# A complex product by three real products in the first spectral layer of an attention + Fourier block

## The chip, the cores and the metric

The kernel runs on one core of a Trainium2 chip. The core has a matrix engine (TensorE, PE in the profile), a vector engine (VectorE, DVE), a scalar engine (ScalarE, ACT), a general engine (GpSimd, POOL) and a queue that starts transfers (SyncE, SP). Each runs its own list of instructions in order, and they wait for each other by semaphores. Matrix products land in PSUM[...]. The metric is the device time of one execution in microseconds (us), lower is better. All times are medians over runs, except where a profiled execution is named.

## The reference

The input is an image of 48 x 48 positions with 768 channels, in float32. A transformer block (attention over all 2304 positions, then a two-layer perceptron) is followed by a spectral layer, and only that layer is touched here. Cut to what matters:

```python
xf = rfft2(x, axes=(1, 2), norm="ortho")              # 48 x 25 frequencies
xf = xf.reshape(B, 48, 25, 8, 96)                     # 8 blocks of 96 channels
xr, xi = real(xf), imag(xf)
o1r = relu(mm(xr, w1[0]) - mm(xi, w1[1]) + b1[0])     # first layer: a complex product
o1i = relu(mm(xi, w1[0]) + mm(xr, w1[1]) + b1[1])
o2r = softshrink(mm(o1r, w2[0]) - mm(o1i, w2[1]) + b2[0], 0.01)   # second layer
o2i = softshrink(mm(o1i, w2[0]) + mm(o1r, w2[1]) + b2[1], 0.01)
y = irfft2(o2r + 1j * o2i, s=(48, 48)) + x
```

`mm` multiplies each block of 96 channels with its own 96 x 96 matrix. So each of the two layers is a product of a complex vector with a complex matrix, block by block.

## The kernel before, in words

The transformer block takes most of the time and is not changed. At its end the perceptron adds its last partial sums into the image (`main`, lines 1018 to 1036, additions on VectorE), and `rows_forward` does the Fourier transform along the rows as matrix products (L1045) and writes the result to DRAM.

The spectral layer starts at L1098. Four PSUM tags, `f`, `l`, `m` and `y`, have two buffers each, one bank a buffer[...]. Weights and constants lie in one large SBUF tile named `shared`, cut into views (L1119 to L1125), and are loaded while the perceptron still ends; the view `a1n` holds the negated imaginary weights, made by one VectorE instruction (L1138).

The frequencies are cut into 14 `Unit`s: two halves of the channels (four blocks of 96 each), and for each half seven groups of column frequencies `k`. A group holds four frequencies, the seventh only one (25 = 6 x 4 + 1). Each unit passes four stages, and each stage is called four times, with `i` = 0 to 3:

- `columns(i)`: the Fourier transform along the columns, for frequency i. Four products of 96 x 96 into PSUM tile `fp`, and a copy to the SBUF tile `xf` (`balanced_copy`: VectorE for even i, ScalarE for odd i).
- `first(i)`: the first complex layer, for block i of the half. It reads all of `xf`, so all four `columns` of the unit come before it. Its real and imaginary inputs `re` and `im` are each 96 partitions by 192 elements (48 for a unit with one frequency). Its output goes to three planes of the tile `o1`: plane 1 the real part, plane 2 the imaginary part, plane 0 the negated imaginary part.
- `second(i)`: the second layer, for frequency i. Eight products into PSUM tile `mp2` (L1211): for each block e, one with planes 1 and 2 of `o1` as the weights, and one with planes 0 and 1. So it reads the output of all four `first` calls, and the last product of each e needs the negated plane. Then VectorE adds the bias (L1215) and makes the clamped copy (L1219), and GpSimd subtracts it (L1220).
- `back(i)`: the inverse transform along the columns. One product with 384 columns into `yp` (L1230), a copy to `y` (`balanced_copy` again), a store to DRAM.

The loop at the end (L1267) puts units into a pipeline. In round r, and for each i, it calls `back(i)` of unit r-3, `second(i)` of unit r-2, `first(i)` of unit r-1 and `columns(i)` of unit r. Below, one such group of up to four calls is a "step". A call does nothing where a unit has only one frequency and i is above 0, except `first`, which runs over blocks. In the last rounds a piece of `rows_back` for the first half of the channels follows each step (two products, an addition of the image, L1254, a store); the rest of `rows_back` comes after the loop, and there each group waits for a 600 KB load `zo` from DRAM.

The matrix engine follows exactly this written order (`manual_schedule`). The order on the other engines is chosen by a scheduler when the program is built.

In `first` before the change, four products are made:

```python
for t, (wr, wi) in enumerate(((a1[:, 0, b], a1n[:, b]), (a1[:, 1, b], a1[:, 0, b]))):
    nc.tensor.matmul(lp[:, t, : self.n], wr, re, start=True, stop=False)   # L1187
    nc.tensor.matmul(lp[:, t, : self.n], wi, im, start=False, stop=True)   # L1188
```

VectorE turns the first half of `lp` into plane 1 (bias and maximum with 0, L1189), ScalarE the second into plane 2 (a Relu, L1193), and GpSimd negates plane 2 into plane 0 (L1197). In float32 every product appears in the profile as two PE records, each with its own weight load.

Of the kernel before, what the change touches and what calls it, by code (L numbers as in the profile page):

```python
# [9 lines left out]
F32 = mybir.dt.float32  # L10
F32R = mybir.dt.float32r
I32 = mybir.dt.int32
AF = mybir.ActivationFunctionType
ALU = mybir.AluOpType
# [5 lines left out]
HW = 48  # L20
# [10 lines left out]
NB = 8  # L31
BS = C // NB
CH = C // 2
# [11 lines left out]
def block_then_afno(  # L45
# [25 lines left out]
    nc = tc.nc  # L71

    def balanced_copy(i, dst, src):
        if i % 2:
            nc.scalar.copy(dst, src)
        else:
            nc.vector.tensor_copy(dst, src)
# [109 lines left out]
    with ExitStack() as flag_scope:  # L187
# [11 lines left out]
        with ExitStack() as att:  # L199
# [115 lines left out]
            def queries_keys_values(qkv):  # L315
# [82 lines left out]
                def seven(product):  # L398

                    bank = [psum.tile([P, G], F32, name=f"m{i}") for i in range(4)]  # L400

                    def made(i, k, first):
                        product(bank[i], k, first)
                        return bank[i]

                    m1 = upool.tile([P, G], F32, name="m1")
                    nc.scalar.copy(m1, made(0, 1, True))
                    u = upool.tile([P, G], F32, name="u")
                    nc.vector.tensor_tensor(u, made(1, 6, True), m1, ALU.add)
                    u7 = upool.tile([P, G], F32, name="u7")  # L410
                    nc.vector.tensor_tensor(u7, made(2, 7, True), u, ALU.add)
                    yield 2, 2, made(3, 5, True), u7
                    yield 1, 1, made(0, 2, False), None
                    yield 2, 1, made(2, 4, False), u
                    yield 1, 2, made(3, 3, False), u

                def queries_and_keys(p, pr, w, ws):
                    b11, b21, t3, b22, t1, t2, t4 = parts_of_tokens(xt, xs)
                    a11, a12, s3, a22 = (w[:, ds(3 * j, 3), i] for i in range(2) for j in range(2))
                    s1, s2, s4 = (ws[:, i] for i in range(3))  # L420
                    pairs_of = {
                        1: (a11, b11), 2: (a12, b21), 3: (s4, b22), 4: (a22, t4),
                        5: (s1, t1), 6: (s2, t2), 7: (s3, t3),
                    }

                    def product(bank, k, first):
                        a, b = pairs_of[k]
                        for c in range(3):
                            nc.tensor.matmul(  # L429
                                bank, a[:, c, :], b[:, c, :], start=(first and c == 0),  # L430
                                stop=(c == 2), skip_group_check=not first,
                            )

                    for i, j, bank, other in seven(product):
                        bias = col((V_QB, V_KB)[i - 1] + pr)
                        o = stage.tile([P, G], F32, name="o")
                        if other is None:
                            nc.scalar.activation(o, bank, AF.Identity, bias=bias)
                        else:
                            nc.vector.scalar_tensor_tensor(o, bank, bias, other, ALU.add, ALU.add)  # L440
                        nc.sync.dma_start(
                            out=(q_d, k_d)[i - 1][pr][:, ds(p * TB + (j - 1) * G, G)], in_=o
                        )
# [77 lines left out]
            with tc.manual_schedule(engines={mybir.EngineType.PE, mybir.EngineType.SP}):  # L521
# [3 lines left out]
                psum = att.enter_context(tc.tile_pool(name="ps_att", bufs=1, space=PSUM))  # L525
# [66 lines left out]
                for n, (pr, c, u) in enumerate(runs):  # L592
# [9 lines left out]
                    for i in range(RUN):  # L602
                        kt = RUN * u + i
                        p = exps[:, (RUN * n + i) % 18]
# [7 lines left out]
                    if pr < NC - 1:  # L612
                        if (c, u) in ((3, 1), (4, 0), (4, 1)):
                            i = 2 * (2 * (c - 3) + u - 1)
# [55 lines left out]
        with tc.tile_pool(name="ps_flag", bufs=1, space=PSUM) as psum, tc.tile_pool(  # L670
            name="ps_early", bufs=2, space=PSUM
# [13 lines left out]
            both = flag_pool.tile([P, 1], F32, name="both")  # L685
# [15 lines left out]
        with tc.If(safe < 1):  # L701
            with ExitStack() as att:
                xnT = main.rearrange("p (c t) -> p c t", c=NC)
                with tc.tile_pool(name="g_ln1", bufs=3) as ln1, tc.tile_pool(
                    name="g_ps_ln1", bufs=2, space=PSUM
# [8 lines left out]
                psum = att.enter_context(tc.tile_pool(name="ps_gen", bufs=2, space=PSUM))  # L714
# [15 lines left out]
                for pr in range(NC):  # L730
# [12 lines left out]
                    for g in range(T // G):  # L743
                        kp = psum.tile([P, G], F32, name="g_kp", tag="m")
                        for c in range(NC):
# [5 lines left out]
                            bias=kb[0:64, pr : pr + 1], scale=HD**-0.5,  # L751
# [6 lines left out]
                    for g in range(T // G):  # L758
                        vp = psum.tile([P, 3, P], F32, name="g_vp", tag="m")
                        for i in range(3):  # L760
                            for c in range(NC):
                                nc.tensor.matmul(
                                    vp[:, i, :], xnT[:, c, ts(3 * g + i, P)], wv[:, c, :],
                                    start=(c == 0), stop=(c == NC - 1),
# [5 lines left out]
                    for sg in range(T // SG):  # L770
# [4 lines left out]
                        for i in range(2):  # L775
                            qp = psum.tile([P, G], F32, name="qp", tag="m")
                            for c in range(NC):
                                nc.tensor.matmul(
                                    qp, wq[:, c, :], xnT[:, c, ds(sg * SG + i * G, G)],
                                    start=(c == 0), stop=(c == NC - 1),  # L780
# [3 lines left out]
                                bias=vec[0:64, V_QB + pr : V_QB + pr + 1],  # L784
# [6 lines left out]
                        for i in range(2):  # L791
                            hp = psum.tile([P, G], F32, name="g_hp", tag="m")
                            for r in range(8):
                                h = sg * 16 + i * 8 + r
                                for j in range(2):
# [4 lines left out]
                                        start=True, stop=True,  # L800
# [7 lines left out]
                        for i in range(2):  # L808
                            wp = psum.tile([P, 24, 16], F32, name="g_wp", tag="m")
                            for r in range(24):  # L810
                                w = i * 24 + r
                                for j in range(2):
# [4 lines left out]
                                        start=True, stop=True,  # L817
# [9 lines left out]
                        for j in range(2):  # L827
                            for qt in range(SG // P):
# [6 lines left out]
                                for g in range(T // G):  # L835
# [3 lines left out]
                                        start=True, stop=True,  # L839
# [16 lines left out]
                                for kg in range(NT // 3):  # L856
# [5 lines left out]
                                    for i in range(3):  # L862
# [3 lines left out]
                                            start=(kt == 0), stop=(kt == NT - 1),  # L866
# [51 lines left out]
    with ExitStack() as mlp:  # L918
        bias = mlp.enter_context(tc.tile_pool(name="mlp_const", bufs=1))
# [5 lines left out]
        psum = mlp.enter_context(tc.tile_pool(name="ps_mlp", bufs=1, space=PSUM))  # L925
# [172 lines left out]
    with ExitStack() as sp:  # L1098
        psum = sp.enter_context(tc.tile_pool(name="ps_spec", bufs=2, space=PSUM))
        cst = sp.enter_context(tc.tile_pool(name="spec_const", bufs=1))  # L1100
        zin = sp.enter_context(tc.tile_pool(name="spec_in", bufs=2))
        mid = sp.enter_context(tc.tile_pool(name="spec_mid", bufs=2))
# [4 lines left out]
        def view(rows, *shape):  # L1107
            nonlocal size
            n = 1
            for k in shape:  # L1110
                n *= k
            size += n
            names = "abc"[: len(shape)]
            dims = dict(zip(names, shape))
            return shared[:rows, ds(size - n, n)].rearrange(
                f"p ({' '.join(names)}) -> p {' '.join(names)}", **dims
            )

        a1 = view(BS, 2, NB, BS)  # L1119
        a2 = view(BS, NB, 2, BS)  # L1120
        d2 = view(2 * HW, NB, BS)
        a1n = view(BS, NB, BS)
        irows = view(4 * KW, 6, P)
        icols = view(2 * HW, 2 * HW)
        cols = view(2 * HW, 2 * HW)  # L1125
        d1 = cst.tile([BS, 2, NB], F32, name="d1")
# [8 lines left out]
            )  # L1135
        nc.sync.dma_start(out=icols, in_=c_icols)
        nc.sync.dma_start(out=irows, in_=c_irows)
        nc.vector.tensor_scalar(a1n, a1[:, 1], -1.0, None, ALU.mult)  # L1138

        z2_h = [z.rearrange("(r k) c -> r k c", k=KW) for z in z2]  # L1140
        NBH = NB // 2
# [1 line left out]
        def by_k(a):  # L1143
            return a.rearrange("p (k h) -> p k h", h=HW)

        class Unit:
# [27 lines left out]
            def first(self, i):  # L1174

                if i == 0:

                    self.o1 = mid.tile([BS, NBH, 4, 3, HW], F32, name="o1")
                b = NBH * self.half + i
                re, im = (  # L1180
                    self.xf[:, i, t, : self.nk, :].rearrange("p k h -> p (k h)") for t in range(2)
                )
                lp = psum.tile([BS, 2, 4 * HW], F32, name="lp", tag="l")
                for t, (wr, wi) in enumerate(
                    ((a1[:, 0, b], a1n[:, b]), (a1[:, 1, b], a1[:, 0, b]))
                ):
                    nc.tensor.matmul(lp[:, t, : self.n], wr, re, start=True, stop=False)  # L1187
                    nc.tensor.matmul(lp[:, t, : self.n], wi, im, start=False, stop=True)  # L1188
                nc.vector.tensor_scalar(  # L1189
                    self.o1[:, i, : self.nk, 1], by_k(lp[:, 0, : self.n]), d1[:, 0, b : b + 1], 0.0,  # L1190
                    ALU.add, ALU.max,
                )
                nc.scalar.activation(  # L1193
                    self.o1[:, i, : self.nk, 2], by_k(lp[:, 1, : self.n]), AF.Relu,
                    bias=d1[:, 1, b : b + 1],
                )
                nc.gpsimd.tensor_scalar(  # L1197
                    self.o1[:, i, : self.nk, 0], self.o1[:, i, : self.nk, 2], -1.0, None, ALU.mult
                )
# [22 lines left out]
            def back(self, i):  # L1222

                if i >= self.nk:
                    return
                zz = self.zz[i]
                if i % 2 == 0:
                    self.y = mid.tile([2 * HW, 2, CH], F32, name="y", bufs=3)
                yp = psum.tile([2 * HW, CH], F32, name="yp", tag="y")
                nc.tensor.matmul(  # L1230
                    yp, icols, zz.rearrange("p n o -> p (n o)"), start=True, stop=True
                )
                balanced_copy(i, self.y[:, i % 2, :], yp)
                if i % 2 or i == self.nk - 1:
                    n = i % 2 + 1
                    nc.sync.dma_start(
                        out=z2_h[self.half][:, ds(self.k0 + i + 1 - n, n), :], in_=self.y[:, :n]
                    )
# [169 lines left out]
```

## Time and profile before

| | |
|---|---|
| median of 3 runs | 2972.0 us (2969.34 to 2973.16) |
| the profiled execution: its own time | 2968.75 us |
| its span in the profile | 2966.9 us |
| PE busy over the span | 2901.3 us (98%) |
| VectorE, ScalarE, GpSimd busy | 1779.2 (60%), 867.4 (29%), 609.4 us (21%) |
| granted TensorE clock | 0.996 |
| first `columns` product | at 2704.24 us |
| last `back` product | at 2924.97 us |

The spectral layer is thus about the last 263 us of the span. Where a row says "x192" it counts PE records, two for each product of the code. A record's mean length overlaps the next one, since matmuls are pipelined: the pace of the engine is read from the starts of records in the timeline, not from their lengths. A row of the timeline holds start, length, engine, source line, operation, tiles and count, and in brackets the idle time of the engine before it and what ended that.

### The profile page before, as it was taken

To read this page: it belongs to the slowest core of one execution; us is meant where nothing else is said; L and a number is where in the kernel's file an instruction comes from. 1 tells how busy PE (TensorE), PEld (TensorE's weight loads), DVE (VectorE), ACT (ScalarE), POOL (GpSimd) and SP (SyncE) were. 2 spreads that over 40 slices of the span, in tenths; PEclk is the share of its full clock that TensorE was granted. 3 is DMA by queue.
4 is the path that set the end of the run, shared out by engine and by line. 5 is a ranking of instruction groups with operands and counts; after the bars stand their busy time and mean duration, and the time that the engine had idled before them with its cause. 6 is when DMAs were issued, how large, how long until landed. Compare 5 with 4: busy or idle time off the path is not lost. (4 is left out here: it accounts for less than half of the span.)

```text
span 2966.9 us, 40951 instructions
## 1 busy us (share of the span) xinstructions
PE 2901.3 (98%) x15771; PEld 1763.4 (59%) x15771; DVE 1779.2 (60%) x2576; ACT 867.4 (29%) x1344; POOL 609.4 (21%) x564
## 2 busy tenths in 40 slices
PE   6999999999999999999999999999999999999998
PEld 4555655655556555555555555555555555557995
DVE  4343237677777777777723666675666566664443
ACT  1011125655555556555500111011111111111210
POOL 2303010000000000000043332343233223312441
PEclk9999999999999999999999999999999999999999
DMA  4423276172452616435242021122112211213235
GB/s 118 152 87 115 94 161 125 26 135 57 83 123 42 141 33 104 103 58 87 62 166 85 32 64 54 54 70 64 51 62 64 75 44 64 64 57 88 78 89 177
DMA packets 202818, 253.04 MB, mean 85 GB/s; under 512 B 21618, under 2 KB 180978, under 8 KB 201078
## 3 DMA queue, kind: packets, MB, share of 16 engines
q1 hardware_dynamic: 202614, 250.32, 33.2%
q8 instruction: 127, 2.08, 0.3%
q14 instruction: 77, 0.63, 0.1%
HBM read 136.40 MB, written 50.14 MB: 63 GB/s over the span
## 5 line engine op out<-in xcount | busy, mean ns | idle before, releaser
L607 DVE TENSOR_TENSOR acc<-acc,main 128x768 f32<-128x768 f32 x576 | 551.8, 958 | 202.0 <-ACT main L550 145.4
L550 ACT ACTIVATE main<-sp 128x768 f32<-128x768 f32 x648 | 522.1, 811 | 155.8 <-PE sp L546 148.6
L546 PE MATMUL sp<-terms,select 64*128 64x384 f32 x1296 | 412.1, 629 | 0.0
L1020 DVE TENSOR_TENSOR main<-o,main 128x384 f32<-128x384 f32 x540 | 298.8, 556 | 40.3 <-PE o L1018 1.8
L958 PE MATMUL h<-shared,w 128*128 128x384 f32 x864 | 296.7, 486 | 0.8 <-issue 0.8
L540 PE MATMUL sp<-shared 64*128 64x384 f32 x1296 | 266.4, 488 | 2.8 <-DVE o L440 2.2
L540 PE MATMUL sp<-qT,kT 64*128 64x384 f32 x1296 | 266.5, 487 | 0.0
L585 POOL TENSOR_TENSOR inverse<-inverse,rden 128x384 f32<-128x384 f32 x36 | 46.3, 1287 | 1029.0 <-DVE rden L582 961.6
L429 PE MATMUL m<-main 128*128 128x384 f32 x756 | 247.1, 488 | 5.5 <-DVE rstd L121 2.6
L958 PEld LDWEIGHTS h<-shared,w 128*128 128x128 f32 x864 | 164.4, 190 | 116.1 <-issue 2.3
L958 PE MATMUL h<-shared,w1s 128*128 128x384 f32 x648 | 226.6, 486 | 0.0
L555 PE MATMUL op<-main,shared 128*64 128x384 f32 x1296 | 221.3, 488 | 0.0
L555 PE MATMUL op<-main,v 128*64 128x384 f32 x1296 | 219.9, 488 | 0.0
L429 PEld LDWEIGHTS m<-main 128*128 128x128 f32 x756 | 142.7, 190 | 107.5 <-issue 8.1
L964 ACT ACTIVATE hT<-c,vec 128x384 f32<-128x384 f32 x108 | 66.4, 615 | 466.2 <-DVE c L970 466.0
L970 DVE TENSOR_TENSOR c<-h,u 128x384 f32<-128x384 f32 x108 | 60.1, 557 | 212.4 <-PE h L958 212.4
L1018 PE MATMUL o<-w,hT 128*128 128x384 f32 x432 | 175.0, 487 | 2.2 <-DVE mv L118 2.0
L1018 PE MATMUL o<-w2s,hs 128*128 128x384 f32 x432 | 174.9, 487 | 1.1 <-DVE hs L153 1.1
L546 PEld LDWEIGHTS sp<-terms,select 64*128 64x128 f32 x1296 | 125.3, 186 | 83.8
L958 PEld LDWEIGHTS h<-shared,w1s 128*128 128x128 f32 x648 | 123.1, 190 | 85.9
L152 POOL TENSOR_TENSOR w1s<-w 128x384 f32<-128x384 f32 x36 | 36.2, 1005 | 611.7 <-PE o L1018 452.6
L555 PEld LDWEIGHTS op<-main,v 128*64 128x64 f32 x1296 | 89.9, 138 | 107.0 <-issue 107.0
(150 smaller groups left out, 3921.6 us busy)
## 6 DMA issues: line engine op xcount, KB each, us to landing
w<-in_mlp_w_dram SPq DMA_DIRECT2D x72, 768.0 KB
terms<-col_parts SPq DMA_DIRECT2D x432, 72.0 KB
terms<-row_hi SPq DMA_DIRECT2D x216, 72.0 KB
terms<-row_lo SPq DMA_DIRECT2D x216, 72.0 KB
main<-in_qkv_w_dram SPq DMA_DIRECT2D x36, 384.0 KB
z<-zt SPq DMA_DIRECT2D x48, 150.0 KB
zo<-z SPq DMA_DIRECT2D x12, 600.0 KB
x<-in_x_dram SPq DMA_DIRECT2D x18, 384.0 KB
```

Source lines behind the costliest of these rows:

```text
L429: nc.tensor.matmul(bank, a[:, c, :], b[:, c, :], start=(first and c == 0), stop=(c == 2), skip_group_check=not first,)
L540: nc.tensor.matmul(sp[:, j, :G], kT[at, ts(kt, P)], qT[at, ts(c, G)], start=True, stop=False,)
L546: nc.tensor.matmul(sp[:, j, :G], select[at, a % 2], ready[pr, c][at, a // 2, b], start=False, stop=True,)
L550: nc.scalar.activation(p, sp[:, :, :G], AF.Exp, scale=HD**-0.5)
L555: nc.tensor.matmul(op[ts(j, 64)], v[:, kt0 + i, ts(j, 64)], ps[i][:, j, :], start=(kt0 + i == 0), stop=(kt0 + i == NT - 1),)
L585: nc.gpsimd.tensor_tensor(inverse, inverse, rden, ALU.add)
L607: nc.vector.tensor_tensor(acc, made[0] if kt == 1 else acc, p, ALU.add)
L958: nc.tensor.matmul(bank[i], a[:, c, :], b[:, c, :], start=(start and c == 0), stop=(c == 2), skip_group_check=not start,)
L964: nc.scalar.activation(h[:, i, ts(k, G)], src, AF.Gelu, bias=col(V_B1 + 2 * n + i))
L970: nc.vector.tensor_tensor(t, src, other, ALU.add)
L1018: nc.tensor.matmul(bank[k], a, b, start=start, stop=True, skip_group_check=not start)
L1020: nc.vector.tensor_tensor(dst, bank[k], dst, ALU.add)
```

## The change

The first layer's four real products become three. With W = (w1[0], w1[1]) the new weights are a1d = w1[1] - w1[0] and a1e = -w1[1] - w1[0], made once by three VectorE instructions in place of one. For each block the sum `both` = re + im is formed on VectorE, and then

- P = w1[0] applied to (re + im), into a new PSUM tile `l1` with one buffer,
- the real part = P + a1e applied to im,
- the imaginary part = P + a1d applied to re.

Since P is needed twice and in PSUM, ScalarE copies it to SBUF (`p_both`), VectorE adds it to both halves of `lp` in one instruction of 384 elements into `pre`, and ScalarE makes both Relus from `pre`. The negation on GpSimd stays. To make room for `l1` in PSUM, `yp` has one buffer in place of two.

```diff
-        a1n = view(BS, NB, BS)
+        a1d = view(BS, NB, BS)
+        a1e = view(BS, NB, BS)
...
-        nc.vector.tensor_scalar(a1n, a1[:, 1], -1.0, None, ALU.mult)
+        nc.vector.tensor_tensor(a1d, a1[:, 1], a1[:, 0], ALU.subtract)
+        nc.vector.tensor_scalar(a1e, a1[:, 1], -1.0, None, ALU.mult)
+        nc.vector.tensor_tensor(a1e, a1e, a1[:, 0], ALU.subtract)
...
+                both = mid.tile([BS, 4 * HW], F32, name="both", bufs=3)
+                nc.vector.tensor_tensor(both[:, : self.n], re, im, ALU.add)
+                l1 = psum.tile([BS, 4 * HW], F32, name="l1", tag="l1", bufs=1)
                 lp = psum.tile([BS, 2, 4 * HW], F32, name="lp", tag="l")
-                for t, (wr, wi) in enumerate(
-                    ((a1[:, 0, b], a1n[:, b]), (a1[:, 1, b], a1[:, 0, b]))
-                ):
-                    nc.tensor.matmul(lp[:, t, : self.n], wr, re, start=True, stop=False)
-                    nc.tensor.matmul(lp[:, t, : self.n], wi, im, start=False, stop=True)
-                nc.vector.tensor_scalar(
-                    self.o1[:, i, : self.nk, 1], by_k(lp[:, 0, : self.n]), d1[:, 0, b : b + 1], 0.0,
-                    ALU.add, ALU.max,
+                nc.tensor.matmul(lp[:, 0, : self.n], a1e[:, b], im, start=True, stop=True)
+                nc.tensor.matmul(lp[:, 1, : self.n], a1d[:, b], re, start=True, stop=True)
+                nc.tensor.matmul(
+                    l1[:, : self.n], a1[:, 0, b], both[:, : self.n], start=True, stop=True
                 )
-                nc.scalar.activation(
-                    self.o1[:, i, : self.nk, 2], by_k(lp[:, 1, : self.n]), AF.Relu,
-                    bias=d1[:, 1, b : b + 1],
-                )
+                p = mid.tile([BS, 4 * HW], F32, name="p_both", bufs=3)
+                nc.scalar.copy(p[:, : self.n], l1[:, : self.n])
+                pre = mid.tile([BS, 2, 4 * HW], F32, name="pre", bufs=3)
+                nc.vector.tensor_tensor(
+                    pre[:, :, : self.n], lp[:, :, : self.n],
+                    p[:, : self.n].unsqueeze(1).to_broadcast([BS, 2, self.n]), ALU.add,
+                )
+                for t in range(2):
+                    nc.scalar.activation(
+                        self.o1[:, i, : self.nk, 1 + t], by_k(pre[:, t, : self.n]), AF.Relu,
+                        bias=d1[:, t, b : b + 1],
+                    )
...
-                yp = psum.tile([2 * HW, CH], F32, name="yp", tag="y")
+                yp = psum.tile([2 * HW, CH], F32, name="yp", tag="y", bufs=1)
```

## The prediction

> **What bounds the kernel now.** I read the page first, then the stretch of the spectral layer: busy time by window, groups by form, and the timeline of single steps. Busy time by window (columns: stretch, length, busy time and instructions of PE, its weight loads, VectorE, ScalarE, GpSimd, then clock, DMA share, GB/s):
>
> ```profile
> 2718.00:2920.00 202.00, 202.00 (x1688) 181.79 (x1687) 95.42 (x208) 39.38 (x97) 81.77 (x102) 1.00 0.28 81
> 2920.00:2967.00 47.00, 38.01 (x114) 20.56 (x112) 16.36 (x30) 0.83 (x2) 0.99 (x1) 0.98 0.67 221
> ```
>
> From 2718 to 2920 us PE is busy the whole time and the others half or less: what PE no longer does there comes off the end, unless something new makes it wait. The chain of waits agrees: through this stretch it is PE alone. The groups by form, from 2640 us on (line, engine, operation, shapes, count; then busy time and mean ns of one):
>
> ```profile
> L1187 PE MATMUL lp<-xf,shared 96*96 96x192 f32 x192 | 47.1, 327 | 0.6 <-ACT xf L75 0.6
> L1188 PE MATMUL lp<-xf,shared 96*96 96x192 f32 x192 | 46.9, 326 | 0.0
> L1197 POOL TENSOR_SCALAR o<-o 96x192 f32<-96x192 f32 x48 | 32.9, 685 | 43.4 <-ACT o L1193 43.4
> L1193 ACT ACTIVATE o<-lp,d 96x192 f32<-96x192 f32 x48 | 20.0, 416 | 134.5 <-DVE o L1189 134.5
> L75 ACT COPY xf<-fp 96x384 f32<-96x384 f32 x24 | 11.1, 464 | 5.2 <-DMA zi<-z 3.1 <-PE fp L1168 2.0
> L1193 ACT ACTIVATE o<-lp,d 96x48 f32<-96x48 f32 x8 | 2.4, 296 | 19.3 <-DVE o L1189 19.3
> ```
>
> Record means overlap, so the pace comes from starts. The end of one round and the start of the next, in the timeline:
>
> ```profile
> 2745.51 0.49 PE L1187 MATMUL lp<-xf,shared 96*96 96x192 f32 x2
> 2746.49 0.49 PE L1188 MATMUL lp<-xf,shared 96*96 96x192 f32 x2
> 2746.82 0.84 PE L1168 MATMUL fp<-shared,zi 96*96 96x96 f32 x8
> 2747.02 0.41 DVE L1189 TENSOR_SCALAR o<-lp,d 96x192 f32<-96x192 f32 x1 [0.29 <-PE lp L1188]
> 2747.46 0.42 ACT L1193 ACTIVATE o<-lp,d 96x192 f32<-96x192 f32 x1 [2.63 <-DVE o L1189]
> 2747.49 0.81 PE L1230 MATMUL yp<-zz,shared 96*96 96x384 f32 x2
> 2747.78 0.46 ACT L75 COPY xf<-fp 96x384 f32<-96x384 f32 x1
> 2747.97 0.68 POOL L1197 TENSOR_SCALAR o<-o 96x192 f32<-96x192 f32 x1 [0.16 <-ACT o L1193]
> 2748.14 1.52 PE L1211 MATMUL mp<-shared,o 96*96 96x96 f32 x16
> 2749.50 0.49 PE L1187 MATMUL lp<-xf,shared 96*96 96x192 f32 x2
> ```
>
> `first(3)` takes 2746.82 - 2745.51 = 1.31 us of PE for 8 records (0.163 each), `columns(3)` 0.67, `back(0)` 0.65, `second(0)` 1.36 (16 records at 0.085); a step is 3.98. PE never waits here. The negated plane is there at 2748.65; `second(0)` needs it for its 15th record, at 2748.14 + 14 x 0.085 = 2749.33. In round 2, which has no `back`, the two meet:
>
> ```profile
> 2718.10 1.61 PE L1211 MATMUL mp<-shared,o 96*96 96x96 f32 x16
> 2718.57 0.68 POOL L1197 TENSOR_SCALAR o<-o 96x192 f32<-96x192 f32 x1 [1.29 <-ACT o L1193]
> 2719.55 0.49 PE L1187 MATMUL lp<-xf,shared 96*96 96x192 f32 x2
> ```
>
> The group is 0.09 longer than the usual 1.52; POOL ends at 2719.25, and counting back two records from 2719.55 the 15th record starts at 2719.38: 0.13 from POOL's end to PE.
>
> [...] The trace: (416 - 296)/144 = 0.83, and the Relu at 2747.46 is followed by a copy 0.32 later, 0.10 under its 0.42. [...]
>
> **The change part by part.**
>
> Removed from PE: 8 records become 6. 48 full calls x 2 x 0.163 = 15.6 us. The 8 calls with 48 columns take 0.084 a record in the timeline, so 8 x 2 x 0.084 = 1.3. Together 17.0 us. Nothing is added on PE.
>
> Load of the others, per step: VectorE `zz` 0.55, `cl` 0.35, `both` 0.36, `pre` 0.56, and on average one 0.55 copy: 2.4 us of a step of now 3.65. ScalarE: the copy of P 0.464 - 192 x 0.00083 = 0.30, two Relus 0.32 apart, one copy: 1.5. No engine comes near PE; what matters is lateness.
>
> `both`: PE needs it 0.65 after a `first` begins. If it were queued behind `zz` and `cl` of the same step, it would be late in each step. In the order in which the built program queues its instructions, VectorE makes the first three of a unit ahead of `zz(0)`, as soon as `xf` is complete, and the fourth right after `cl(0)`, three steps early. Cost nothing, covered by `back` and `second`.
>
> One bank for `yp` and `l1`: `back(i)` now waits for the copy of `back(i-1)`, which ends some 1.4 us after that product began (2747.49 to 2748.89 above), against a step of 3.65. P is copied by 1.5 us after `first` begins, and `l1` is needed again a step later. In the last rounds `back` is 1.94 apart, still over 1.4. Nothing.
>
> The new chain into `second(0)`. Let 0 be the start of `first(3)`. PE: the three products end their pace at 0.98, `columns(3)` at 1.65, `back(0)` at 2.30; `second(0)` wants the negated plane at 2.30 + 1.19 = 3.49. ScalarE: the last product's record pair starts at 0.65 and ends 0.49 later, P is copied at 1.18 to 1.48; VectorE adds from 1.52 to 2.08. In the built queue ScalarE's next instruction is not the Relu but the copy of `columns(3)`: it waits for PE (0.98 + 0.84 = 1.82, start 1.86, end 2.32). The Relus follow at 2.23 and 2.55 and end at 2.97; GpSimd starts 0.09 later and ends at 3.74; PE goes on at 3.87. So PE waits 0.38 where before 0.55 was to spare (2749.33 - 2748.65 - 0.13). This holds for rounds 3 to 7 and 9 to 12: round 8 follows a unit with 48 columns (shorter instructions), and from round 13 on a `rows_back` piece of 1.3 us lies between. 9 x 0.38 = 3.4. Round 2 has no `back`, so the plane is wanted at 2.84: 1.03, less the 0.09 already there[...]; I take 1.1. Behind PE's wait stand all later products, so these 4.5 us go straight onto the end. Bounds: nothing, if Relus from SBUF are quicker and the copy isn't in the way; and, if each Relu costs 0.1 more and a `both` (0.36) delays the negation, 9 x 0.94 + 1.7 = 10.2. I take 4.5.
>
> The three weight instructions: two of them stand in VectorE's queue at about 2657 us, where it then idles 3.31 us (before the row at 2663.60) and 1.4 us more find room, also if the weights land a microsecond late. The third stands where the old one did (2666.01), 0.96 in place of 0.55 (the 768-wide row L607 has 958 ns). Behind it VectorE had 0.16 idle before L152, and PE waits for L153 right after:
>
> ```profile
> 2670.12 0.56 DVE L152 TENSOR_TENSOR hs<-hT 128x384 f32<-128x384 f32 x1 [0.16 <-PE o L1018]
> 2671.76 0.88 PE L1018 MATMUL o<-w2s,hs 128*128 128x384 f32 x2 [1.10 <-DVE hs L153]
> ```
>
> So 0.41 - 0.16 = 0.25 us of loss. The tail after 2925 us starts earlier as a whole: its `zo` loads follow the stores of `y`, which follow PE.
>
> Sum: 17.0 - 4.5 - 0.25 = 12.2 us off. The profiled execution took 2968.75 (span 2966.9), so it would take 2956.5; the median of the runs is 3.25 higher, 2972.0, which gives 2959.8, or 2960.
>
> **The rivals.**
>
> No waits: the Relus come early enough, or the Relu-and-negate chain is faster than its rows. For it: all instructions are short, VectorE idles. Against: the copy in front of the Relus. Time 2972.0 - 17.0 + 0.25 = 2955. Chance 0.14.
>
> The waits eat most: GpSimd is held off at each boundary by `both`, the Relus are slower from SBUF, and other waits appear at the starts of rounds. At the upper bound the time is 2965.5, a little more and it is within 0.2% of before (6 us, about what a measurement of this kernel can tell from no change). Chance 0.12.
>
> Slower: `both` comes late in each step after all. Behind `zz` and `cl` it would be ready at about 1.6 after the start of `first` (0.2 + 0.55 + 0.11 + 0.36 + 0.36) for a need at 0.65, and 48 waits of 1.0 us against 17 us saved give 2972 + 31 = 3003. It decides from 0.36 us a step (17.0/48). For it: `both` is a new wait in front of PE; against: the built order has it one step ahead or more. Chance 0.04.
>
> The change doesn't do what it says: PE's pace is set by something that stays (weight loads, 182 us of 202), and fewer records bring no time. Against: the 48-column records run at 0.084 with the same weight loads. Time 2972. Chance 0.06.
>
> **How the numbers follow.** The likeliest case has 0.64 and gives 2960. The range, 2954 to 2967, runs from no waits (2955, less a microsecond for the spread of the runs) to the upper bound of the waits (2965.5) and a little over; it leaves out the last two rivals and part of the second. Faster by over 0.2%: 0.64 + 0.14 + half of 0.12 and a little more, 0.86; same 0.10; slower 0.04.
>
> **What would show it.** Right: 288 full PE records of the first layer in place of 384, at a pace of 0.163; a step of 3.65 us; at the start of rounds 3 to 7 and 9 to 12 a wait of PE for GpSimd of about 0.4, in round 2 of about 1.1; the copy `xf` between the P copy and the Relus. Wrong: PE idle in every step (before `l1` for VectorE, before `yp` for a copy), a step over 3.98, or a `both` that lasts 0.7 and more beside GpSimd.

## The result, and the profile after

The kernel after takes 2961.42 us (median of 8 runs, 2956.03 to 2965.74), the kernel before on the same chip 2972.3 (8 runs, 2969.34 to 2984.55). The ratio is 0.9961, with a 95% interval from 0.9947 to 0.9974: some 11 us less, and between 7.7 and 15.8. The forecast was 2960. The profiled execution of after is the longest of its eight, 2965.74 us (span 2963.9); more on that stands under the second experiment.

In the changed file the lines are: `columns` L1173, `both` L1189, the three products of `first` L1192 to L1194, the copy of P L1198, `pre` L1200, the Relus L1205, the negation L1209, `second` L1223 (its VectorE instructions L1227 and L1231, its GpSimd one L1232), `back` L1242, the weight instructions L1141 to L1143.

Busy time by window of after, the first of the two windows shown of before (columns: stretch, length, busy time and count of PE, its weight loads, VectorE, ScalarE, GpSimd, then clock, DMA share, GB/s):

```profile
2718.00:2920.00 202.00, 197.66 (x1629) 174.30 (x1629) 118.75 (x266) 76.06 (x212) 87.86 (x106) 0.99 0.30 86
```

PE was busy for all of the 202 us before; now it idles 4.34 of them. VectorE rose from 95 to 119 us and ScalarE from 39 to 76, and neither is near the length of the window. What PE waits for, from 2640 us to the end (line of the waiting instruction, what it waits for, then total, times and longest, in us):

```profile
PE mp L1223 <- POOL o L1209: 3.9, 10, 0.4
...
PE mp L1223 <- ACT o L1205: 0.4, 2, 0.2
PE o L1018 <- DVE main L1020: 0.3, 1, 0.3
```

The four rows left out were there before too, with nearly the same totals (before and after: `zo` 5.6 and 4.9, `zt` 3.9 and 4.4, `hs` 1.1 and 1.1, `xf` 0.6 and 0.6). These three are new: ten waits for the negation, two for a Relu, one for `main`. No row names `both` or the copy of `yp`. A wait counts only PE's idle time; how much the work moves is more, and is read from the starts. The groups by form of after:

```profile
L1205 ACT ACTIVATE o<-pre,d 96x192 f32<-96x192 f32 x96 | 38.4, 447 | 17.4 <-DVE pre L1200 17.4
L1209 POOL TENSOR_SCALAR o<-o 96x192 f32<-96x192 f32 x48 | 34.5, 719 | 69.5 <-ACT o L1205 34.6 <-issue 27.9 <-POOL zz L1232 7.1
L1192 PE MATMUL lp<-xf,shared 96*96 96x192 f32 x96 | 24.6, 339 | 0.6 <-ACT xf L75 0.6
```

L1193 and L1194 have 96 records too, so 288 records with 192 columns stand where 384 stood. A Relu takes 447 ns from `pre` in place of 416 from PSUM, the negation 719 on average in place of 685. The start of a round in after, which answers to the timeline shown of before:

```profile
2752.41 0.32 ACT L1198 COPY p_both<-l 96x192 f32<-96x192 f32 x1 [1.56 <-PE l L1194]
2752.76 0.55 DVE L1200 TENSOR_TENSOR pre<-lp,p_both 96x384 f32<-96x384 f32 x1 [0.31 <-ACT p_both L1198]
2753.09 0.47 ACT L75 COPY xf<-fp 96x384 f32<-96x384 f32 x1 [0.36 <-PE fp L1173]
2753.47 0.80 ACT L1205 ACTIVATE o<-pre,d 96x192 f32<-96x192 f32 x2
2753.54 1.35 PE L1223 MATMUL mp<-shared,o 96*96 96x96 f32 x14
2754.34 0.76 DVE L1189 TENSOR_TENSOR both<-xf 96x192 f32<-96x192 f32 x2
2754.35 0.88 POOL L1209 TENSOR_SCALAR o<-o 96x192 f32<-96x192 f32 x1 [0.82 <-ACT o L1205]
2755.29 0.41 PE L1223 MATMUL mp<-shared,o 96*96 96x96 f32 x2 [0.40 <-POOL o L1209]
```

The chain runs down the rows: the copy of P, `pre`, the copy `xf` that stands ahead of the Relus, the Relus, the negation, and PE. `second(0)` starts at 2753.54, and the next `first` at 2755.53, 1.99 later; with nothing to wait for it takes 1.36. So this boundary costs 0.63 us, where the forecast had 0.38. The two sums `both` of the next unit start together with the negation, which takes 0.88 here.

A length that the chances of other stages don't touch runs from the start of the last `columns` of round 1 to the start of the last `back`, both read from PE's rows in the timeline: 207.39 us before (2717.42 to 2924.81, the first of its two records), 198.69 after (2723.79 to 2922.48). I call it the long stretch. It is 8.7 shorter. Its two ends, first in before, then in after:

```profile
2717.42 0.84 PE L1168 MATMUL fp<-shared,zi 96*96 96x96 f32 x8
2924.81 0.81 PE L1230 MATMUL yp<-zz,shared 96*96 96x384 f32 x2
2723.79 0.84 PE L1173 MATMUL fp<-shared,zi 96*96 96x96 f32 x8
2922.48 0.81 PE L1242 MATMUL yp<-zz,shared 96*96 96x384 f32 x2
```

### The profile page after: what moved, and what is told of

The parts are those of the page before. It is cut to its first block, busy times and chain, and to the rows that moved or that the text cites. A ratio compares the mean times of both kernels' runs of the same rounds, so it can differ in the third digit from the quotient of the medians.

```text
span 2963.9 us, 40921 instructions
## 1 busy us (share of the span) xinstructions
PE 2894.5 (98%) x15659; PEld 1753.2 (59%) x15659; DVE 1803.1 (61%) x2634; ACT 903.7 (30%) x1456; POOL 611.3 (21%) x564
## 5 line engine op out<-in xcount | busy, mean ns | idle before, releaser
L958 PE MATMUL h<-shared,w 128*128 128x384 f32 x864 | 296.8, 487 | 0.8 <-issue 0.8
L958 PEld LDWEIGHTS h<-shared,w 128*128 128x128 f32 x864 | 164.4, 190 | 116.2 <-issue 2.3
L958 PE MATMUL h<-shared,w1s 128*128 128x384 f32 x648 | 226.6, 486 | 0.0
L1018 PE MATMUL o<-w,hT 128*128 128x384 f32 x432 | 175.0, 487 | 2.1 <-DVE mv L118 2.0
L1018 PE MATMUL o<-w2s,hs 128*128 128x384 f32 x432 | 174.8, 486 | 1.1 <-DVE hs L153 1.1
L958 PEld LDWEIGHTS h<-shared,w1s 128*128 128x128 f32 x648 | 123.1, 190 | 85.9
L540 PEld LDWEIGHTS sp<-shared 64*128 64x128 f32 x1296 | 118.4, 187 | 59.6 <-issue 23.1
```

The lines of the kernel that those rows point to most:

```text
L540: nc.tensor.matmul(sp[:, j, :G], kT[at, ts(kt, P)], qT[at, ts(c, G)], start=True, stop=False,)
L958: nc.tensor.matmul(bank[i], a[:, c, :], b[:, c, :], start=(start and c == 0), stop=(c == 2), skip_group_check=not start,)
L1018: nc.tensor.matmul(bank[k], a, b, start=start, stop=True, skip_group_check=not start)
```

## The experiments

Each was timed beside the kernel before on the same chip; e1 to e4 ran on one chip, e5 to e7 on another.

| kernel | median us | ratio to before | 95% interval | long stretch us |
|---|---|---|---|---|
| before | 2972.1 to 2972.4 | 1 | | 207.39 |
| after | 2961.42 | 0.9961 | 0.9947 to 0.9974 | 198.69 |
| e1 three of four products | 2952.91 | 0.9932 | 0.9918 to 0.9946 | 191.87 |
| e2 after again | 2962.06 | 0.9958 | 0.9944 to 0.9973 | 198.69 |
| e3 first and columns early | 2954.53 | 0.9938 | 0.9926 to 0.9951 | 192.53 |
| e4 Relus swapped | 2955.25 | 0.9943 | 0.9930 to 0.9956 | 193.74 |
| e5 `both` with one buffer | 2959.05 | 0.9956 | 0.9943 to 0.9970 | 197.10 |
| e6 before with side parts | 2974.92 | 1.0009 | 1.0000 to 1.0017 | 207.39 |
| e7 e3, weights on GpSimd | 2957.97 | 0.9951 | 0.9933 to 0.9969 | 192.53 |

The times scatter with the clock that each run was granted, which is on record for 103 of the runs. A straight line through these, with one level for each kernel, falls by 2.6 us for each 0.001 of clock. At equal clock it puts e1 16.5 us under before, e3 15.9, e7 15.7, e4 13.4, e5 11.9 and after 9.9 (both sets of its runs together), and e6 2.1 above it, each with a standard error of 0.5 to 1.0. This is an estimate, made from other data than the long stretch, and the kernels come out in nearly the same order.

The theory: the change saves 17 us on PE, and a chain that has grown too long gives some of it back at the starts of rounds. The rivals are in the expectations.

**e1. One product less, nothing added** (to the kernel before)

```diff
-                    nc.tensor.matmul(lp[:, t, : self.n], wr, re, start=True, stop=False)
-                    nc.tensor.matmul(lp[:, t, : self.n], wi, im, start=False, stop=True)
+                    nc.tensor.matmul(lp[:, t, : self.n], wr, re, start=True, stop=(t == 1))
+                    if t == 0:
+                        nc.tensor.matmul(lp[:, t, : self.n], wi, im, start=False, stop=True)
```

> The kernel before with one of the four products of each first call left out (the second product of the imaginary part, so the imaginary part lacks w1[0] applied to im); nothing is added, the weights are prepared as before, yp keeps two banks. It prices the saving on PE alone. Theory (PE's pace is set by its records): a step of 3.65 to 3.66 us in place of 3.98, PE idle nowhere at the round boundaries, 17.0 us less than before: ratio 0.9943 (0.993 to 0.995). Rival (pace set by something that stays, so part of the saving of the kernel after came from elsewhere): step above 3.8, less than 10 us off. If it comes out at 11 us off like the kernel after, then the new waits of the kernel after cost nothing.

Measured: 19.2 us under before by the medians; the interval goes from 16 to 24 and holds the 17.0. The long stretch gives the sharper number: 207.39 - 191.87 = 15.5, where the forecast's 17.0, less 1.3 for the four calls of round 1 that lie ahead of the stretch, leaves 15.7. PE's waits in this kernel are the four of before (`zo` 6.1, `zt` 3.9, `hs` 1.1, `xf` 0.6) and one in the tail, 0.7 for an addition there; none is in `second`. What follows: PE's pace is set by its records, the rival that it is set by something that stays is out, and the kernel after loses 198.69 - 191.87 = 6.8 us of that saving inside the spectral layer.

**e2. The kernel after, unchanged**

> The kernel after, unchanged, beside the others on the same chip. Theory: 10 to 13 us under before (ratio 0.9956 to 0.9966), PE's waits for GpSimd at the round boundaries again 0.6 us each in rounds 3 to 6 and 9 to 12, about 1.0 in rounds 2 and 7, 7 us in all. The stretch at half clock behind PE's idle 4 us at the start of the spectral layer is chance: its length (about 13 us in the first profile of after, about 4 in that of before) should differ from one profile to the next. Rival (that stretch belongs to the changed kernel): again 10 us or more, and then the kernel loses about 4 us there in every run.

Measured: 10.0 us under before, and the long stretch is the same to the hundredth. PE's waits for GpSimd are those of the first profile, 3.9 us in ten. The clock at the start of the spectral layer is not. Windows of after's first profile (columns as above; the third column from the right is the clock):

```profile
2716.00:2720.00 4.00, 4.00 (x20) 3.70 (x19) 1.46 (x3) 1.22 (x4) 0.69 (x1) 0.50 0.02 7
2720.00:2724.00 4.00, 4.00 (x31) 3.96 (x30) 1.57 (x3) 2.42 (x8) 0.69 (x1) 0.83 0.28 78
```

and of the same kernel here:

```profile
2716.00:2720.00 4.00, 4.00 (x25) 3.81 (x23) 1.45 (x3) 1.42 (x4) 0.69 (x1) 0.65 0.11 43
2720.00:2724.00 4.00, 4.00 (x39) 4.00 (x38) 2.13 (x4) 2.71 (x9) 1.37 (x2) 1.00 0.31 80
```

PE idles some 4 us before its first `columns` product; about there the clock falls to half, for 13.7 us in the first profile and 10.2 in this one. The rival had foretold 10 us or more here, so this run alone doesn't put it out. All nine profiles together do: the stretch is in every one, and its length, listed in the last section, doesn't go with the change, since 13.7 and 10.2 occur in two kernels made from before (e1, e6) and 3.4 in two made from after (e3, e4).

The two profiled executions of after lie 4.3 and 5.9 us above their medians, and have the lowest granted clock of their sets (0.993). This one stretch is only a part of that: from the first `columns` product to the last `columns` of round 1 they take 15.37 and 13.91 us, against 11.13 in e3 and e4. By windows of 5 us, the first of the two has another 27 us at half clock ahead of 2650 us, in code that the change doesn't touch; before has 17 there. I therefore compare kernels by the long stretch: it begins after the half-clock stretch, in before, after and e1 to e5 the clock over it is 1.00, and e6 and e7 repeat the lengths of before and e3 to the hundredth.

**e3. `first` and `columns` ahead of `back` and `second`**

```diff
-                    for stage, lag in (("back", 3), ("second", 2), ("first", 1), ("columns", 0)):
+                    for stage, lag in (("first", 1), ("columns", 0), ("back", 3), ("second", 2)):
```

> The kernel after with another order of the four calls of a step: first, columns, back, second in place of back, second, first, columns. The same work; between first(3) and the second(0) that needs its negated plane there now lie columns, back, second and the next first and columns. Theory (the 7 us of PE's waits come from the long chain behind first(3) and nothing else): no wait of PE for GpSimd at any round boundary, steps still 3.66, 6 to 7 us less than after (ratio to before 0.9935 to 0.994, 2953 to 2955). Rival (the waits come from GpSimd and the copy being busy at the boundary, or the order of the steps brings a new wait: first(0) of the next round then needs the last xf copy and its sum within 2 us): the waits move to first(0), and the time is that of after or above.

Measured: 7.5 us under after by the medians of the same chip, 6.2 by the long stretch (198.69 - 192.53). PE's waits:

```profile
PE rps L1263 <- DMA zo<-z: 5.8, 5, 2.8
PE fp L1173 <- ACT zt L75: 4.2, 1, 4.2
PE lp L1192 <- ACT xf L75: 1.1, 2, 0.6
PE o L1018 <- DVE hs L153: 1.1, 1, 1.1
PE o L1018 <- DVE main L1020: 0.4, 1, 0.4
```

All waits for the negation and for a Relu are gone. One new one came, 0.56 us for the last `xf` ahead of `first(0)` in round 2, where no `second` lies between; that is nearly all that is left between this kernel and e1 (192.53 - 191.87 = 0.66). So the 6.8 us were the chain, and work placed between its two ends hides it. The rival saw the new wait, but it comes once, not in each round. With 17.6 us under before it has the lowest median of the versions that compute the whole layer; e4's interval overlaps with its own, and by the long stretch e3 is 1.2 us ahead of e4.

**e4. The Relus swapped, imaginary plane first**

```diff
-                for t in range(2):
+                for t in (1, 0):
```

> The kernel after with the two Relus in the other order: the imaginary plane first, so that the negation can start one Relu (0.35 us) earlier. Same instructions. Theory: the wait at the boundaries of rounds 3 to 6 and 9 to 12 falls from 0.63 to 0.2 to 0.35, that of rounds 2 and 7 to about 0.65, so 3 to 4 us less than after (ratio to before about 0.995). Rival (the wait is set by the negation being held off by the two sums both on VectorE): the negation then starts earlier but ends as late, and nothing is gained; or the real plane comes last and PE waits for that Relu instead: second(0) needs plane 1 of the last block for its 13th record already, 0.17 earlier.

Measured: 6.8 us under after by the medians, 4.95 by the long stretch. More than expected. A boundary in its timeline:

```profile
2741.80 0.80 ACT L1205 ACTIVATE o<-pre,d 96x192 f32<-96x192 f32 x2
2741.87 1.62 PE L1223 MATMUL mp<-shared,o 96*96 96x96 f32 x16
2742.34 0.69 POOL L1209 TENSOR_SCALAR o<-o 96x192 f32<-96x192 f32 x1 [0.47 <-ACT o L1205]
2742.68 0.61 DVE L1189 TENSOR_TENSOR both<-xf 96x192 f32<-96x192 f32 x2
2743.33 0.49 PE L1192 MATMUL lp<-xf,shared 96*96 96x192 f32 x2
```

The negation starts 0.54 after the first Relu, where it started 0.88 after it; and it takes 0.69 in place of 0.88, because the sums now come later than its start. Together that is 0.34 + 0.19 = 0.53 of the 0.63. What is left is 0.10: `second(0)` takes 2743.33 - 2741.87 = 1.46 in place of 1.36. Only rounds 2 and 7 still wait, now for the Relu that comes last (0.24 and 0.16 of idle time). The theory had the first half, and took the second for unchanged.

**e5. One buffer for `both`**

```diff
-                both = mid.tile([BS, 4 * HW], F32, name="both", bufs=3)
+                both = mid.tile([BS, 4 * HW], F32, name="both", bufs=1)
```

> The kernel after with one buffer for the sum both in place of three. In VectorE's built queue the two sums that stood at each round boundary, beside the negation, then lie one step later each, between cl and pre. Theory (the pair of sums stretches the negation from 0.69 to 0.88 there): the negation takes 0.69 to 0.72, PE's shift at the boundaries falls from 0.63 to about 0.45, 1.5 to 2 us less than after; in the steps nothing is added, because a sum still ends before the next first begins. Rival A (the stretch has another cause): the negation stays at 0.88 and the waits are as before. Rival B (with one buffer the sum is late in each step): PE waits for VectorE ahead of the third product in 36 steps, 10 us or more above after.

Measured: 2.4 to 3.0 us under the two medians of after, within their spread; 1.6 by the long stretch. Its boundary:

```profile
2748.18 0.68 POOL L1209 TENSOR_SCALAR o<-o 96x192 f32<-96x192 f32 x1 [0.82 <-ACT o L1205]
2748.91 0.41 PE L1223 MATMUL mp<-shared,o 96*96 96x96 f32 x2 [0.20 <-POOL o L1209]
```

With no sum on VectorE beside it the negation takes 0.68, and PE's wait falls from 0.40 to 0.20. That holds for all eight such boundaries (8 x 0.20 = 1.6). So the pair of sums did cost 0.2 us at each. Rival A is out; so is rival B: PE waits nowhere for `both`, even with one buffer.

**e6. The side parts alone, in the kernel before**

```diff
+        a1d = view(BS, NB, BS)
+        a1e = view(BS, NB, BS)
...
+        nc.vector.tensor_tensor(a1d, a1[:, 1], a1[:, 0], ALU.subtract)
+        nc.vector.tensor_tensor(a1e, a1n, a1[:, 0], ALU.subtract)
...
-                yp = psum.tile([2 * HW, CH], F32, name="yp", tag="y")
+                yp = psum.tile([2 * HW, CH], F32, name="yp", tag="y", bufs=1)
```

> The kernel before with two side parts of the change alone: yp with one bank, and three VectorE weight instructions in place of one (a1d and a1e are made but not used). Theory: no wait of PE for the copy of yp anywhere, the spectral layer exactly as before (7.5 of PE's stall-free steps of 3.98); in the perceptron's tail PE waits for the additions of main inside the last but one group, so that the time from the h group at about 2651 us to the first zp product is 34.2 to 34.4 us in place of 33.59: 0.6 to 0.8 us slower, too little for the comparison of times (ratio 0.999 to 1.0015). Rival: one bank for yp costs a wait per step, then 56 waits show and the time is 5 us or more above before.

(The bracket on 7.5 steps in it has no meaning; nothing rests on it.) Measured: 2.5 us above before, with an interval from 0 to 5. The long stretch is 207.39, the very number of before: one bank for `yp` costs nothing, and no wait for it shows. From the `h` group at 2649.80 to the first `zp` product at 2684.86 it is 35.06 us, 1.47 more than the 33.59 of before. That is twice what I expected, since the built program put the two new instructions among the additions of `main` in two groups rather than one. In its timeline L1141 (0.94) starts at 2655.65 and four such additions follow it, and L1142 (0.94) starts at 2666.34 between two others. Each costs PE about 0.74: behind the first, starts of L1018 and L958 that lie 0.64 to 0.65 apart in before are 0.87, 1.05 and 0.75 apart, since the products of L1018 go into PSUM tiles that these additions free.

**e7. e3 with the weight instructions on GpSimd**

```diff
-        nc.vector.tensor_tensor(a1d, a1[:, 1], a1[:, 0], ALU.subtract)
-        nc.vector.tensor_scalar(a1e, a1[:, 1], -1.0, None, ALU.mult)
-        nc.vector.tensor_tensor(a1e, a1e, a1[:, 0], ALU.subtract)
+        nc.gpsimd.tensor_tensor(a1d, a1[:, 1], a1[:, 0], ALU.subtract)
+        nc.gpsimd.tensor_scalar(a1e, a1[:, 1], -1.0, None, ALU.mult)
+        nc.gpsimd.tensor_tensor(a1e, a1e, a1[:, 0], ALU.subtract)
```

> The kernel after with first and columns ahead of back and second in each step, and with the three weight instructions on GpSimd, which is idle in the perceptron's tail. Theory: as with the order alone (no wait for the negation), and the time from the last but one h group to the first zp product back to 33.6 us: 0.6 to 0.8 us under the order alone, in total 7 to 8 us under after (ratio to before 0.9930 to 0.9938). Rival: the delay in the perceptron's tail has another cause (the weights' arrival, or a GpSimd instruction holding VectorE off), then 34.2 to 34.4 stays.

Measured: the trace is as the theory says; the times can't tell. From 2650.75 (`h`) to 2684.46 (`zp`) it is 33.71 us, against 34.36 in e3, and PE's wait for `main` is gone. The three instructions take 2.13, 1.81 and 1.82 us there, and nobody waits for them. But its six runs spread from 2949.36 to 2964.60, so the median says nothing on 0.65 us. It lies 3.4 above that of e3, and only 3.5 to 4.1 under the two of after, where 7 to 8 were expected. Its runs were granted less clock, 0.9943 on average against 0.9952 in e3; at equal clock, by the line under the table, e7 and e3 are 0.2 apart with a standard error of 1.2. Its profile has the longest tail of all, 43.3 us from the last `back` to the last product, against 38.8 before and 38.1 and 41.3 in the two profiles of after, with a granted clock of 0.88 from 2940 us on. Whether an earlier end of the spectral layer makes this tail longer in itself, or only its half-clock stretches do, these runs don't settle.

## Why the prediction was right

By its own steps:

- **Removed from PE, 17.0 us.** Right. Four calls in round 1 go from 1.98 to 1.65 us at full clock (e4), which is 1.3, and e1 shows 15.5 in the long stretch: 16.8.
- **The load of the others.** Right: nowhere does PE wait for VectorE in a step, and a step takes 3.66 us (`columns` groups start at 2748.55 and 2752.21 in the timeline of after) against the 3.65 forecast. My estimates for the new instructions held nearly: by after's profile `both` takes 0.375 us on average (0.36 estimated; 0.355 in e5), `pre` 0.554 (0.56), the copy of P 0.315 (0.30).
- **`both` costs nothing.** Right for PE, and e5 shows room to spare. What it does to the negation is below.
- **One bank for `yp` and `l1` costs nothing.** Right, shown for `yp` by e6 and for both by the lack of a wait.
- **The new chain into `second(0)`, 4.5 us.** The place, the mechanism and the order of ScalarE's queue were right; the size was not: 6.8. Counted from the start of `first(3)` (2751.24) the Relus start at 2.23, as forecast. Then the negation starts at 3.11 (3.06 forecast; the Relus take 0.447 in place of 0.416), and ends at 3.99 (3.74 forecast), because it takes 0.88. The step that failed there is "GpSimd starts 0.09 later and ends at 3.74": it took the 0.68 of a negation that has no `both` beside it. That a `both` might delay the negation was a guess of mine that no row of before showed; it entered the upper bound, but not the central value of these rounds, although the built order had the pair of sums right there. e5 prices that omission at 0.20 a round.
- **Round 7 at 0.38.** Wrong: it costs 1.00. In round 6 the unit in `columns` has one frequency, so its steps 1 to 3 have no `columns`, and the cover ahead of `second(0)` is 0.67 shorter. The forecast treated round 8, after the short unit's `first`, and overlooked its `columns`. After, PE at that boundary:

```profile
2796.69 0.81 PE L1242 MATMUL yp<-zz,shared 96*96 96x384 f32 x2
2797.33 1.18 PE L1223 MATMUL mp<-shared,o 96*96 96x96 f32 x12
...
2799.45 0.41 PE L1223 MATMUL mp<-shared,o 96*96 96x96 f32 x2 [0.37 <-POOL o L1209]
```

  The next `first` starts at 2799.69; 2799.69 - 2797.33 is 2.36 in place of 1.36, and no L1173 row stands ahead of L1242. The missing 0.67 of cover is partly made up: the copy `xf` isn't in the Relus' way (0.1), and the negation takes 0.69 there (0.19 less): 0.63 + 0.67 - 0.1 - 0.19 = 1.0. Round 2, forecast at 1.1, has 0.99 (1.08 by the starts, less the 0.09 that was there before). Added up: 8 x 0.63 + 1.00 + 0.99 = 7.0, close to the 6.8 of the difference.
- **The weight instructions, 0.25 us.** The size was off (0.6 to 0.8) and the place too. The third instruction, said to cost 0.25, costs nothing: the wait for L153 is 1.10 in both profiles. The two said to find room cost it all. VectorE of after:

```profile
2661.00 0.94 DVE L1143 TENSOR_TENSOR shared<-shared 96x768 f32<-96x768 f32 x1
2661.86 2.11 DVE L1020 TENSOR_TENSOR main<-o,main 128x384 f32<-128x384 f32 x4
```

  The idle 3.31 us that was to take them in comes only after these additions; L1142 stands at 2660.07, one addition ahead of these rows. Each of these additions frees a PSUM tile for a product of PE, and with 0.55 and 0.94 us put among them PE idles 0.35 us for `main`, ahead of the product at 2662.47.
- **The sum.** 16.8 - 6.8 - 0.7 = 9.3, against 12.2 forecast and 10.9 and 10.0 measured in two comparisons, whose intervals hold both; at equal clock the estimate is 9.9. The gross saving and the mechanism of the loss were right; the loss was 2.8 us larger. By these parts the time would be 2963, so that 2961.4 came out so near to the forecast of 2960 is in part luck. Of the rivals, "the waits eat most" named two of the causes, Relus slower from SBUF (447 ns against 416) and the sums beside the negation (0.88 us against 0.68), but not round 7 and not the place of the weight instructions; "no waits" and "`both` late in each step" found nothing in the trace, and "no effect" fell with e1.

## What to carry to other kernels

Where a change trades work on the full engine for a longer chain through the idle ones, cost the chain at the places where its cover is thinnest (here the start of a round, and the rounds where a stage is missing), with the durations that its members have beside what the queues put next to them, not with their means. Then look whether the order of the stages can give it cover: here one line of order brought back 6.2 of 6.8 us. An engine's mean idle time says nothing of room at one place: in e6 a weight instruction of 0.94 us cost PE some 0.7 among the additions that it waited for; in after one of 0.94 that stood in the next group, in the place of one of 0.55, cost nothing.

## What the runs showed of the hardware that I had not expected

The half-clock stretch comes in steps. Where PE idles 3.6 to 4.4 us at the start of the spectral layer, the clock falls to 0.50 and stays there for 3.4 us (e3, e4), 6.8 (before), 10.2 (e2, e5, e6, e7) or 13.7 (after, e1), read from windows of one and four microseconds: one to four times 3.4 us. PE is busy for most of it, in after for 12.4 of the 13.7 us. What decides how long it lasts, no run here shows: the same kernel had 13.7 and 10.2. At half clock a step of round 1 takes 3.20 us (in after, from 2716.45 to 2719.65) in place of 1.65. With 13.7 us of it in place of 3.4, rounds 0 and 1 take 4.2 us longer (15.37 against 11.13), more than half of what the chain cost that the experiments were about.

The sums `both` and the negation can lengthen each other. In after, where the pair of sums and the negation start within 0.01 us (2754.34 and 2754.35), the negation takes 0.88 and the pair 0.76; in e4, where the negation has a lead of 0.34, both overlap for 0.35 us and neither grows (0.69 and 0.61). What decides between the two, no run here shows. PE's wait behind the negation says the same: 0.40 in after, 0.20 in e5, where no sum stands beside it and the negation takes 0.68.
